# Group norm and attention on one core: the first input loaded, normalised and projected by channel chunks

## The chip, the cores and the metric

The kernel runs on one core of a Trainium2 chip. The metric is the device time of one execution in microseconds. "Span" is the length of the profiled execution; it is about 1.7 us shorter than the time of the same execution. PE is TensorE, DVE VectorE, ACT ScalarE, POOL GpSimd, SP SyncE.

## The reference

```python
# x: (4, 512, 48, 48) f32, 32 groups of 16 channels, 8 heads of 64
hn  = group_norm(x, gn_scale, gn_bias)                 # eps 1e-5
qkv = einsum('oc,bchw->bohw', qkv_w, hn) + qkv_b       # 1536 x 512, then f16
q, k, v = ...                                          # per head: 64 x 2304
w   = softmax(einsum('bhct,bhcs->bhts', q * s, k * s)) # s = 1 / sqrt(sqrt(64))
a   = einsum('bhts,bhcs->bhct', w, v)
out = x + einsum('oc,bchw->bohw', proj_w, a) + proj_b
```

## The kernel before

The 512 channels are four chunks c of 128 partitions; the 2304 positions are five blocks j, four of 512 and one of 256. A q or k chain of a head pair is, for one block, an accumulation over the four chunks. Each chunk is one step: two matmuls with 64 output rows, each of which the trace records as two passes (f32; 160 records for the 40 steps of pair 0). PE and DVE keep the order in which the program is written. The order of ACT, POOL and SP is chosen by the scheduler of the build. The front of the program, before attention starts:

```python
def load_x(b, j, engines):                   # block by block, all chunks of a block
    o, n = QBLOCKS[j]
    for c in range(NC):
        t = xpool.tile([P, n], F32, tag=f"x{c}_{j}", name=f"x_{b}_{c}_{j}")
        engines[c % len(engines)].dma_start(t, x[b, bass.ts(c, P), o : o + n])
        hn[b, c, j] = t
for j in range(NQ):
    load_x(0, j, (nc.sync, nc.scalar))
...
nc.gpsimd.dma_start(brow..., qkv_b[:, 2 * NC :]...)       # 512 values of 4 bytes
for part, engine in ((1, nc.sync), (0, nc.scalar), (2, nc.sync)):
    engine.dma_start(wqkv[:, :, cols], ...)               # 1 MB each
nc.gpsimd.partition_broadcast(bv, brow[0:1, :], P)        # bias of v on all partitions
...
nc.gpsimd.memset(gmat, 1.0 / GROUP)
for sign, base in ((1, 0), (-1, GROUP - 1)):
    nc.gpsimd.affine_select(out=gmat, in_=gmat, ...)      # gmat: 1/16 within a group
...
def group_mean(b):       # bn_aggr per chunk, PE: gmat x mean, DVE: mean, dev, dev^2, var
def group_var(b):        # PE: gmat x var; DVE: + eps; POOL: pow -0.5; DVE: ga, mga, gb
def norm(b, j):          # DVE: x * ga + gb, in place, per chunk
...
for j in range(NQ):
    stats(0, j)                              # DVE bn_stats
group_mean(0)
group_var(0)
norm(0, 0)
for j in range(NQ):
    if j + 1 < NQ:
        norm(0, j + 1)
    for part in (1, 0):                      # k chain, then q chain of block j
        for p in qk_chain(0, part, j):
            p[1]()
for i in range(0, NT, 2):                    # then the v chains, then attention
    for p in v_chain(0, 0, i):
        p[1]()
```

## Time and profile before

| | before |
|---|---|
| time, median of 4 runs | 1709.38 us (1708.64 to 1709.68) |
| span of the profiled execution (a run of 1708.11 us) | 1706.4 us |
| first q/k step on PE | 24.68 us |
| first v matmul on PE | 58.37 us |
| from there to the end | 1648.0 us |

After the first q/k step PE hardly rests any more. So the time of the first v matmul is the figure to watch: it contains all that the change touches. The prediction shows the views of this profile. In its chain of waits a piece is counted from the end of the one before, so v stands there at 58.53; PE's timeline has the start itself:

```profile
58.37 31.25 PE L712 MATMUL pv<-wqkv,x 128*64 128x256 f32 x288
```

The granted clock of this trace is on record from 30.18 on. It is 1.00 or 0.50 of full speed, and its nine changes after that lie whole multiples of 3.413 us apart (87 of them from 30.18 to 327.14, then two to 333.97). So windows of 3.41 us on that grid are used below, and "half clock" is a window at 0.50. Ahead of 30.18 the speed is read from the steps.

### The profile page before, as it was taken

What the parts mean: (1) busy time and instruction counts of PE and PEld (TensorE: products, weight loads), DVE (VectorE), ACT (ScalarE), POOL (GpSimd) and SP (SyncE); (2) the same over time, 40 slices, a digit from 0 to 9 for tenths busy, and PEclk for the clock granted to TensorE, in tenths of its full rate; (3) what the DMA queues carried; (4) which work ended last, traced back from release to release, by engine and by line L of the source; (5) the groups of instructions that cost most, each with busy time, mean ns of one, the idle gap of its engine ahead of it and who ended that gap; (6) DMA issues with size and microseconds to landing.
All of it is one profiled execution on the core that took longest, in us unless ns stands there. A gap on an engine that the chain in (4) does not pass through costs nothing.

```text
span 1706.4 us, 28896 instructions
## 1 busy us (share of the span) xinstructions
PE 1631.4 (96%) x11876; PEld 719.9 (42%) x11876; DVE 1019.8 (60%) x1124; ACT 1232.9 (72%) x1297; POOL 345.0 (20%) x497
## 2 busy tenths in 40 slices
PE   4999999899999999899999999999999999999896
PEld 1533444254333543445433344355534334444344
DVE  5256555876555555767556555676655555566564
ACT  0077787767787786767787777876777888877882
POOL 1001112111211211231211211122111221123331
PEclk9999999999999999999999999999999999999999
DMA  6001002200000012430100001343010000024233
GB/s 204 1 19 26 11 15 77 64 8 17 14 11 13 17 26 73 141 101 18 48 14 10 14 17 22 100 132 95 14 44 11 14 17 14 14 78 115 69 106 114
DMA packets 93774, 81.89 MB, mean 48 GB/s; under 512 B 50880, under 2 KB 58944, under 8 KB 93632
## 3 DMA queue, kind: packets, MB, share of 16 engines
q1 hardware_dynamic: 91488, 76.51, 16.3%
q10 hardware_dynamic: 1968, 3.41, 0.6%
q8 instruction: 95, 1.56, 0.4%
q14 instruction: 47, 0.39, 0.1%
q0 software_dynamic: 176, 0.02, 0.0%
HBM read 60.44 MB, written 19.16 MB: 47 GB/s over the span
## 4 chain that ended last, share of the span: by engine, by line
PE 87%; DVE 5%; DMA 3%; ACT 3%; issue 2%; POOL 0%; SPq 0%; DVEq 0%; POOLq 0%; ACTq 0%
PE pqk L672 29%; PE ps L831 17%; PE av L856 17%; PE pv L712 14%; PE pr L760 7%; PE sl L904 3%; ACT p L838 3%; DVE acc L888 2%; DVE st L589 1%; DMA out_dram<-r 1%; DMA x<-x_dram 1%; DMA r<-x_dram 1%; DVE x L628 1%; DVE avx L865 0%; DMA ib<-row 0%
## 5 line engine op out<-in xcount | busy, mean ns | idle before, releaser
L838 ACT ACTIVATE p<-ps 128x1024 f16<-128x1024 f32 x1296 | 1231.6, 1027 | 427.5 <-PE ps L831 426.9
L672 PE MATMUL pqk<-x,wqkv 128*64 128x512 f32 (+1 forms) x2560 | 540.8, 555 | 6.1 <-DVE x L628 2.6
L888 DVE TENSOR_TENSOR acc<-acc,p 128x3072 f16<-128x3072 f16 x270 | 481.7, 1784 | 81.7 <-ACT p L838 81.0
L831 PE MATMUL ps<-q,k 64*128 64x512 f16 (+1 forms) x2880 | 364.4, 360 | 15.3 <-ACT p L838 14.9
L856 PE MATMUL av<-p,v 128*64 128x512 f16 (+1 forms) x2880 | 362.1, 365 | 0.1
L672 PEld LDWEIGHTS pqk<-x,wqkv 128*64 128x64 f32 x2560 | 176.4, 138 | 247.1 <-issue 188.2
L941 POOL TENSOR_SCALAR in<-sums 128x8 f32<-128x8 f32 (+1 forms) x160 | 115.0, 719 | 803.0 <-DMA sums<-slx 796.5
L712 PE MATMUL pv<-wqkv,x 128*64 128x256 f32 x2304 | 267.7, 380 | 1.4 <-DVE x L628 1.4
L831 PEld LDWEIGHTS <-k 64*128 64x128 f16 x2880 | 107.7, 94 | 291.6 <-issue 245.4
L856 PEld LDWEIGHTS <-v 128*64 128x64 f16 x2880 | 131.6, 109 | 212.4 <-issue 168.9
L963 POOL TENSOR_TENSOR att<-avx,ib 128x512 f16<-128x512 f32 (+1 forms) x78 | 119.8, 1536 | 421.5 <-DMA ib<-row 378.2
L712 PEld LDWEIGHTS pv<-wqkv,x 128*64 128x64 f32 x2304 | 160.0, 137 | 93.9 <-issue 7.2
L888 DVE TENSOR_TENSOR acc<-p,p 128x3072 f16<-128x3072 f16 x80 | 140.2, 1753 | 62.1 <-ACT p L838 61.6
L681 DVE TENSOR_SCALAR q<-pqk,bqkv 128x512 f16<-128x512 f32 (+1 forms) x80 | 55.8, 697 | 140.2 <-PE pqk L672 140.2
L720 DVE TENSOR_TENSOR v<-pv,bv 128x512 f16<-128x512 f32 x72 | 49.8, 691 | 135.5 <-PE pv L712 135.5
L681 DVE TENSOR_SCALAR k<-pqk,bqkv 128x512 f16<-128x512 f32 (+1 forms) x80 | 55.8, 697 | 125.0 <-PE pqk L672 125.0
L760 PE MATMUL pr<-a,whi 128*128 128x512 f32 (+1 forms) x304 | 121.0, 404 | 3.9 <-POOL a L752 3.3
L760 PE MATMUL pr<-a,wlo 128*128 128x512 f32 (+1 forms) x304 | 113.7, 380 | 0.0
L771 DVE SCALAR_TENSOR_TENSOR r<-pr,bproj,r 128x512 f32<-128x512 f32 (+1 forms) x80 | 55.3, 696 | 86.2 <-PE pr L760 75.6
L752 POOL CAST a<-att 128x512 fp32r<-128x512 f16 (+1 forms) x75 | 64.3, 891 | 88.0 <-PE pr L760 87.7
L904 PE MATMUL sl<-acc,ones 128*64 128x512 f16 (+1 forms) x576 | 67.4, 350 | 13.0 <-DVE avx L865 12.8
L760 PEld LDWEIGHTS pr<-a,whi 128*128 128x128 f32 x304 | 57.2, 188 | 41.6 <-issue 21.9
(56 smaller groups left out, 385.3 us busy)
## 6 DMA issues: line engine op xcount, KB each, us to landing
r<-x_dram SPq DMA_DIRECT2D x64, 256.0 KB, 2.9
out_dram<-r SPq DMA_DIRECT2D x64, 256.0 KB, 2.5
ib<-row SPq DMA_DIRECT2D x126, 128.0 KB, 3.0
x<-x_dram SPq DMA_DIRECT2D x56, 256.0 KB, 3.2
x<-x_dram ACTq DMA_DIRECT2D x8, 256.0 KB, 7.1
wqkv<-qkv_wT_dram SPq DMA_DIRECT2D x2, 1024.0 KB, 8.1
sums<-slx SPq DMA_DIRECT2D x128, 2.0 KB, 2.1
r<-x_dram SPq DMA_DIRECT2D x16, 128.0 KB, 2.2
```

The lines of the kernel that those rows point to most:

```text
L672: nc.tensor.matmul(pw[0][lo : lo + D, :n], wqkv[:, c, w0 + lo : w0 + lo + D], hn[b, c, j], start=(c == 0), stop=(c == NC - 1),)
L681: nc.vector.tensor_scalar(qk[g][part][:, o : o + n], pw[0][:, :n], bqkv[:, col : col + 1], SCALE, ALU.add, ALU.mult,)
L712: nc.tensor.matmul(pw[0][lo : lo + D, a, :], hn[b, c, i * P // QB][:, at + lo : at + lo + D], wqkv[:, c, 2 * C + half * C // 2 :][:, : C / ...
L752: engine.tensor_copy(at32[b, j][:, c, :n], atts[b * NPAIR + c][:, o : o + n])
L760: nc.tensor.matmul(ps[:, :n], w[:, c, bass.ts(m, P)], at32[b, j][:, c, :n], start=(c == 0 and i == 0), stop=(c == NC - 1 and i == 1),)
L831: nc.tensor.matmul(ps[:, h, a * n : (a + 1) * n], kt[rows, bass.ts(i, P)], qt[rows, o : o + n], start=True, stop=True,)
L838: nc.scalar.activation(pt[:, r], ps, AF.Exp)
L856: nc.tensor.matmul(av[0][lo : lo + D, :n], vv[b, pr // 2][:, i, pr % 2 * P + lo : pr % 2 * P + lo + D], pt[:, r, h, a * n : (a + 1) * n], ...
L888: nc.vector.tensor_tensor(acc[g, j][0], before, pt, ALU.add)
L904: nc.tensor.matmul(sl[lo : lo + D, :n], ones16, t[:, r, h, a * n : (a + 1) * n], start=(i == 0), stop=(i == len(steps) - 1),)
L941: nc.gpsimd.tensor_scalar(t, sm, limit, None, op)
L963: nc.gpsimd.tensor_tensor(atts[g][:, o : o + n], avx.pop((g, j))[:, :n], ib[:, :n], ALU.mult)
```

## The change

The intent: PE waits 24.7 us because the group norm is started only when all of x has arrived. Groups lie within a chunk, so a chunk's norm needs nothing of the other chunks. The change loads chunk 0 first and takes its statistics, coefficients and norm. It then carries six open accumulation chains (five k, one q, in six PSUM banks) one step forward with each chunk. The norm of the first x goes to ScalarE, the bias broadcast is written further down, and small slices of the k and q weights are loaded ahead.

```diff
+    load_w(1, slice(0, P), nc.scalar)
+    for c in range(NC):
+        for j in range(NQ):
+            load_x(0, j, c, (nc.sync, nc.scalar)[j % 2])
+        if c == 0:
+            load_w(0, slice(0, P), nc.scalar)
+    load_w(2, slice(0, C), nc.sync)
+    load_w(1, slice(P, C), nc.scalar)
+    load_w(0, slice(P, C), nc.sync)
 ...
+    bv = const.tile([P, C], F32, name="bv")              # was above gmat
+    nc.gpsimd.partition_broadcast(bv, brow[0:1, :], P)
 ...
+    def norm_chunk(b, c):
+        ga, gb = coef["ga", b], coef["gb", b]
+        for j in range(NQ):
+            t = hn[b, c, j]
+            nc.scalar.activation(
+                t, t, AF.Identity, bias=gb[:, c : c + 1], scale=ga[:, c : c + 1]
+            )
 ...
+    def coefficients(c):
+        for j in range(NQ):
+            stats(0, j, (c,))
+        group_mean(0, (c,))
+    six = [(1, j) for j in range(NQ)] + [(0, 0)]
+    banks = [
+        ps_s.tile([P, 2, QB], F32, tag="ps", name=f"ps_{i}") for i in range(3)
+    ]
+    chains = [qk_steps(0, *a, banks[i // 2][:, i % 2, :]) for i, a in enumerate(six)]
+    coefficients(0)
+    group_var(0, (0,))
+    for c in range(NC):
+        norm_chunk(0, c)
+        for i, step in enumerate(chains):
+            step(c)
+            if c + 1 < NC and i == 1:
+                coefficients(c + 1)
+            if c + 1 < NC and i == 3:
+                group_var(0, (c + 1,))
+    for j in range(1, NQ):                               # the other four q chains
+        for p in qk_chain(0, 0, j):
+            p[1]()
```

The cuts: group mean and variance take a list of chunks and write columns of shared tiles; qk_steps is the body of qk_chain with a bank given from outside.

## The prediction

> **What bounds the kernel now.** I read the page first (busy shares, slices, chain), then the chain of waits and the timeline of the first 80 us, because the change touches nothing after that. TensorE is busy for 96% of the 1706.4 us span. The only long stretch without it is the front: the first of 40 slices shows PE at 4 tenths, all others at 8 or more. So the front is worth about 24.7 us, and after it PE's order fixes the rest: a microsecond gained or lost before PE turns continuous should move the end by about one.
>
> The page's busy line and two rows of the slices:
>
> ```profile
> PE 1631.4 (96%) x11876; PEld 719.9 (42%) x11876; DVE 1019.8 (60%) x1124; ACT 1232.9 (72%) x1297; POOL 345.0 (20%) x497
> ...
> PE   4999999899999999899999999999999999999896
> ...
> PEclk9999999999999999999999999999999999999999
> ```
>
> The chain of waits, cut to 0 to 80 us (start, duration, what):
>
> ```profile
> 2.18 7.71 DMA x<-x_dram
> ...
> 9.90 6.80 DMA x<-x_dram
> ...
> 16.73 2.59 DVE st L589 x6
> 19.32 0.65 DVE mv L594 x4
> ...
> 20.11 0.57 PE gmean L596 x2
> ...
> 22.39 1.07 POOL rstd L614
> ...
> 24.68 33.85 PE pqk L672 x160
> 58.53 21.58 PE pv L712 x199
> ```
>
> Read it so: x arrives until 16.7, the last statistics end at 19.3, the group coefficients take from 20.11 to 24.05, one norm 0.6, then PE has 33.85 us of q/k chains for pair 0 and goes on with v at about 58.45. That last time is what the change has to beat.
>
> The timeline of GpSimd shows something the chain does not, as it is hidden in before:
>
> ```profile
> 5.64 0.37 POOL L552 TENSOR_SCALAR_AFFINE_SELECT gmat<-gmat 128x128 f32<-128x128 f32 x1 [0.28 <-POOL fine L570]
> 13.18 0.80 POOL L529 PARTITION_BROADCAST bv<-brow  x1 [7.17 <-DMA brow<-qkv_b_dram]
> 13.84 0.46 POOL L552 TENSOR_SCALAR_AFFINE_SELECT gmat<-gmat 128x128 f32<-128x128 f32 x1
> ```
>
> The group matrix gmat is finished at 14.30 only, because its second select stands behind the broadcast of a bias row whose load lands at 13.1. Every group mean needs gmat.
>
> Last, PE's busy time in windows of 3.41 us (columns: window, its length, PE busy, PEld, DVE, ACT, POOL, PE clock, DMA, GB/s):
>
> ```profile
> 323.73:327.14 3.41, 1.55 (x10) 0.55 (x10) 3.31 (x4) 3.41 (x5) 0.00 (x0) 1.00 0.18 53
> 327.14:330.55 3.41, 2.00 (x10) 0.69 (x11) 3.41 (x6) 0.29 (x1) 0.00 (x0) 0.50 0.00 0
> 330.55:333.97 3.42, 3.34 (x18) 0.91 (x12) 2.69 (x7) 3.24 (x4) 0.00 (x0) 0.50 0.04 1
> 374.93:378.34 3.41, 1.85 (x22) 1.03 (x23) 2.20 (x3) 0.65 (x1) 0.00 (x0) 1.00 0.02 5
> ```
>
> I laid these windows over the whole span: four with PE busy for 0.84 to 1.60 us were followed by half clock, none with 1.85 or more was (the end aside). Half clock ended after a window of 3.34 or 3.41 us busy, and did not end after one of 2.00.
>
> [...] the first six 512-column steps (two 64-row halves, two passes each) come every 1.71 us, the later ones every 0.857, turning at 30.2, though the page's clock row prints 9 there. [...] here 47% busy was already too little. [...] Before's table load is 1.28 us; no norm runs on ScalarE in before[...]. [...] the bias row, 512 values of 4 bytes: 8.6 us to landing, and 592 packets under 512 B in the first 70 us.
>
> **The change part by part.** I compared the two built programs instruction by instruction on each engine.
>
> (1) Loads. x comes chunk by chunk, with small slices of the k and q weights ahead. No byte less. Each load waits for the one eight places earlier (before: SP waited 9.7 us for x). Chunk 0 lies in the first six loads; before's first eight were in by about 10 us, so its statistics end near 9. That gains nothing, since gmat comes at 14.3: **the source moves the broadcast down, but GpSimd's built order still has it ahead of the second select.** The first group mean runs at about 14.35 instead of 20.11. Its coefficients need 24.05 - 20.11 = 3.93 us, as before (waits and fixed costs, not columns): 18.28.
>
> (2) The norm of the first x goes from VectorE to ScalarE. 20 norms (16 of 0.48 and 4 of 0.34 us pitch, 9 us) leave VectorE, all beside PE. ScalarE gets 20[...]. But ScalarE issues 12 loads first; its last waits for the 15th. In before the third weight load was gated alike and was issued at 17.3. Table load 1.28: ScalarE is free at about 18.6. [...] **PE starts at about 19.4 instead of 24.68, 5.3 us earlier.**
>
> (3) PE's work is the same: ten chains, 8 x 3.43 + 2 x 1.72 = 30.9 us warm. It is only cut: six chains (5.5 steps of 0.857 = 4.7 us per chunk) run in four portions, four q chains follow unbroken (3 x 3.43 + 1.72 = 12.0). Three more pairs of tiny group matmuls (0.6 us each, cold) come in.
>
> (4) New waits: VectorE works in order, and the code puts the statistics of chunk c+1 after the coefficients of c, group mean after PE step 2, group variance after step 4. So a loop of dependences forms, per chunk: statistics 4 x 0.638 + 0.33 = 2.88, aggregate 0.2, group mean until PE goes on about 0.5, two PE steps 1.71, variance to coefficients 24.04 - 21.51 = 2.53. Sum **7.8 us per chunk, against 4.7 us of PE work**. PE waits about 0.5 us before the mean and 1.5 us before the next chunk; the rest is tiny matmuls.
>
> Sum: chunk 0 starts at 19.4. It is cold: 3.43 + 0.6, two steps partly cold 2.6, 2.53[...] make 9.9, so chunk 1 starts at about 29.3 or, where the clock turns early, 28.5. Two rounds of 7.8: chunk 3 at 44.5 (28.5 to 29.3 + 15.6). Its steps 4.7, then 12.0: v starts at about **61.4 against 58.45, 3 us later**. The head start of 5.3 is spent: in the loop PE idles or does tiny matmuls for about 9 us, and cold steps still cost 2 to 3 us as before.
>
> (5) Clock. In the loop a 3.41 us window that catches both pauses has 1.7 us of PE work, next to the 1.60 that throttled and the 1.85 that did not. A trip costs up to 1.7 us, some of it hidden in the pauses. I add 1 us. After the front nothing differs: later batches keep VectorE norms and the same pools.
>
> **Rivals.** A, the intent works: PE starts 5 us earlier and stays fed, v starts at 53 to 54, time 1704 to 1705. For it: the loads and ScalarE are fast enough. Against: the statistics of the next chunk stand behind this one's coefficients. I give it 7%. B, my loop with a warm clock: 1711 to 1714, 55%. C, loop plus throttling once or twice: 1714 to 1717, 23%. D, PE never warms in the loop, as its pauses keep every window below what ends half clock: a chunk costs 10.7 us, v starts 10 to 12 us late, 1720 to 1722. For it: 61% busy did not wake it in before. Against: cold, PE would be over 80% busy. 12%. E, gmat or ScalarE's start moves by 2 us with the bias row's or the 15th load's landing: it shifts B or C by 1 to 2 us. Small rest: something unseen.
>
> **Range and chances.** The middle of B and C is 1709.55 + 3 + 1 = 1713.5 us. Below, A alone goes under 1709; above, D ends near 1721. The three runs before span 1 us. A range from 1709.0 to 1719.5 should hold it 8 times in 10. Two per cent is 34 us, more than the whole front before PE starts: same 0.985, faster 0.005, slower 0.01.
>
> **What would show it.** gmat's second select near 14.3 behind the broadcast; the first group mean just after; ScalarE's first norm near 18.6 after the table load; first q/k matmul near 19.4; statistics of each chunk starting right after the coefficients of the one before; chunk starts 7.8 us apart; v from about 61.4. I am wrong if the second q/k portion starts within 6 us of the first (A), if steps stay at 1.71 us past 35 us (D), or if PE's pauses after 62 us change.

## The result

The changed kernel takes 1718.96 us (median of 4 runs, 1718.32 to 1721.22), 9.6 us more than before. A ratio, here and below, is the mean time of one kernel's fast runs over that of the other's of the same rounds, so it is not quite the ratio of the medians: 1.0059, 95% interval 1.0042 to 1.0076. By the 2% measure that is "same". In the trace the first v matmul moved from 58.37 to 68.91 us, 10.5 us, and the span grew by 10.7; from there to the end it is 1648.2 us against 1648.0. So all of the loss lies in the front.

The page's busy line and the slices of PE:

```profile
PE 1636.3 (95%) x11888; PEld 722.4 (42%) x11888; DVE 1014.9 (59%) x1128; ACT 1246.6 (73%) x1317; POOL 343.3 (20%) x500
...
PE   4999999899999999989999999999999999999796
```

At this scale nothing is to be seen: the first slice is 4 tenths as before. ACT has gained 20 norms (13.7 us). The chain of waits, cut to 0 to 80 us, tells more (start, duration, what):

```profile
3.80 8.94 DMA brow<-qkv_b_dram
...
14.05 0.60 PE gmean L617 x2
...
16.27 5.65 issue
21.92 0.60 POOL rstd L635
...
23.12 0.82 ACT x L654
...
23.99 3.68 PE ps L698 x8
...
32.35 2.72 DVE st L602 x5
...
39.41 2.72 DVE st L602 x5
```

The loads of x have left the chain, as intended, and the first group mean runs at 14.05 instead of 20.11. Then 5.65 us pass in which the chain shows "issue", that is, no releaser that the profile knows, before GpSimd's power. So the first q/k step starts at 23.99, only 0.7 us earlier than before. After that, up to the last chunk, the chain goes through VectorE's statistics for each chunk, not through PE.

GpSimd's timeline of the changed kernel (in brackets the idle time before, and its end):

```profile
13.54 0.46 POOL L560 TENSOR_SCALAR_AFFINE_SELECT gmat<-gmat 128x128 f32<-128x128 f32 x1
21.92 0.59 POOL L635 TENSOR_TENSOR rstd<-veps,mhalf 128x1 f32<-128x1 f32 x1 [7.92 <-issue]
```

The power's input was there at 16.26, and GpSimd had been idle since 14.00. The packed trace holds two MODIFY_POOL_CONFIG records at 13.92 and 13.96, between the two lines (the views of the profile leave them out), and two more at 5.97 and 6.00, ahead of the broadcast. What GpSimd does in this hole no instruction of the profile shows. In before the same records stand at 14.23 and 14.26 and the same gap of 8.09 us stood ahead of the power, but there VectorE's input ended it (22.30, power at 22.39), so the profile named VectorE and the hole did not show.

PE's timeline, the starts of chunks 1 and 2, the last chunk and v, then its busy time in two clock windows (columns as in the prediction):

```profile
33.25 1.94 PE L698 MATMUL ps<-x,wqkv 128*64 128x512 f32 x8 [0.88 <-ACT x L654]
...
40.31 1.94 PE L698 MATMUL ps<-x,wqkv 128*64 128x512 f32 x8 [0.87 <-ACT x L654]
...
47.37 1.08 PE L698 MATMUL ps<-x,wqkv 128*64 128x512 f32 x4 [0.87 <-ACT x L654]
49.39 3.33 PE L698 MATMUL ps<-x,wqkv 128*64 128x512 f32 x8 [0.95 <-DVE k L707]
53.66 1.51 PE L698 MATMUL ps<-x,wqkv 128*64 128x512 f32 x8 [0.94 <-DVE k L707]
55.98 1.08 PE L698 MATMUL ps<-x,wqkv 128*64 128x512 f32 x4 [0.80 <-DVE k L707]
...
68.91 21.32 PE L743 MATMUL pv<-wqkv,x 128*64 128x256 f32 x196
```

```profile
46.37:49.79 3.42, 1.60 (x8) 0.42 (x8) 0.84 (x2) 3.29 (x5) 0.00 (x0) 1.00 0.01 2
49.79:53.20 3.41, 2.93 (x8) 0.60 (x4) 1.19 (x2) 0.13 (x1) 0.00 (x0) 0.50 0.00 0
```

Chunks 1, 2 and 3 start 7.06 us apart. In the last one PE waits three times 0.8 to 0.95 us for VectorE, which reads a finished k chain out of PSUM. The window with the wait for ScalarE at the chunk's start and the first of these three has 1.60 of 3.42 us of PE work, and the next one runs at half clock: the step pair after 49.39 takes 3.33 us instead of 1.94 (in e5 the same pair, after the same wait, takes 1.94).

### The profile page after: what moved, and what is told of

It is laid out like the page before. It is cut to its first block, busy times and chain, and to the rows that moved or that the text cites. A ratio compares the mean times of both kernels' runs of the same rounds, so it can differ in the third digit from the quotient of the medians.

```text
span 1717.1 us, 28955 instructions
## 1 busy us (share of the span) xinstructions
PE 1636.3 (95%) x11888; PEld 722.4 (42%) x11888; DVE 1014.9 (59%) x1128; ACT 1246.6 (73%) x1317; POOL 343.3 (20%) x500
## 4 chain that ended last, share of the span: by engine, by line
PE 87%; DVE 5%; ACT 2%; DMA 2%; issue 2%; POOL 1%; SPq 0%; DVEq 0%; ACTq 0%; POOLq 0%
PE pqk L698 27%; PE ps L862 17%; PE av L887 17%; PE pv L743 14%; PE pr L791 7%; PE sl L935 3%; ACT p L869 2%; DVE acc L919 2%; DVE st L602 1%; PE ps L698 1%; DMA r<-x_dram 1%; DMA out_dram<-r 1%; DMA brow<-qkv_b_dram 1%; DVE x L645 0%; DVE avx L896 0%
## 5 line engine op out<-in xcount | busy, mean ns | idle before, releaser
L698 PE MATMUL pqk<-x,wqkv 128*64 128x512 f32 (+1 forms) x2464 | 518.1, 551 | 3.3 <-DVE k L707 2.0
L698 PEld LDWEIGHTS pqk<-x,wqkv 128*64 128x64 f32 x2464 | 168.9, 137 | 229.6 <-issue 177.2
L919 DVE TENSOR_TENSOR acc<-p,p 128x3072 f16<-128x3072 f16 x80 | 140.3, 1753 | 61.4 <-ACT p L869 60.8
L707 DVE TENSOR_SCALAR k<-pqk,bqkv 128x512 f16<-128x512 f32 (+1 forms) x75 | 52.3, 697 | 114.7 <-PE pqk L698 114.7
```

Of the source, the lines that this page charges most:

```text
L698: nc.tensor.matmul(pw[0][lo : lo + D, :n], wqkv[:, c, w0 + lo : w0 + lo + D], hn[b, c, j], start=(c == 0), stop=(c == NC - 1),)
L707: nc.vector.tensor_scalar(qk[g][part][:, o : o + n], pw[0][:, :n], bqkv[:, col : col + 1], SCALE, ALU.add, ALU.mult,)
L919: nc.vector.tensor_tensor(acc[g, j][0], before, pt, ALU.add)
```

## The experiments

The theory after the trace: three causes, each in the front. (F) GpSimd's hole between the broadcast and the first power (7.92 us after the second select, 5.65 of them with the input there) sets the start. (S) VectorE's order, with the statistics of a chunk behind the coefficients of the one before, sets the distance of the chunks. (W) In the last chunk PE waits for the reader of the neighbour bank, and the clock drops. The rivals: ScalarE's norms, the loads, or the chunk-wise form itself.

All eleven kernels (there is no e6 on record) gave results that agree with the reference. "First step" and "first v" are from the profiled execution of each; times are medians. The runs of before beside each call had medians of 1710.44, 1710.91, 1710.29 and 1709.96 us (11 runs each).

| kernel | first step | first v | time us | ratio to before (95%) |
|---|---|---|---|---|
| before | 24.68 | 58.37 | 1709.38 | |
| the change | 23.99 | 68.91 | 1718.96 | 1.0059 (1.0042 to 1.0076) |
| e1_bias_dma | 19.18 | 61.93 | 1713.87 | 1.0022 (1.0010 to 1.0034) |
| e2_last_order | 24.97 | 64.96 | 1716.48 | 1.0038 (1.0025 to 1.0051) |
| e3_ahead | 24.96 | 62.82 | 1713.04 | 1.0018 (1.0006 to 1.0031) |
| e4_norm_dve | 25.05 | 75.02 | 1726.97 | 1.0096 (1.0082 to 1.0111) |
| e5_block_loads | 24.41 | 67.40 | 1718.78 | 1.0044 (1.0031 to 1.0057) |
| e7_reordered | 14.21 | 53.08 | 1704.66 | 0.9964 (0.9950 to 0.9977) |
| e9_reordered_warm | 16.75 | 52.56 | 1706.43 | 0.9968 (0.9954 to 0.9982) |
| e8_before_warm | 29.30 | 60.27 | 1707.66 | 0.9981 (0.9968 to 0.9995) |
| e10_before_warm_short | 27.96 | 61.81 | 1708.92 | 0.9980 (0.9964 to 0.9996) |
| e11_before_bias_dma | 24.30 | 58.25 | 1711.07 | 1.0007 (0.9995 to 1.0020) |
| e12_before_bias_warm | 26.02 | 56.99 | 1706.74 | 0.9989 (0.9975 to 1.0004) |

### e1_bias_dma: no broadcast on GpSimd

```diff
-    nc.gpsimd.partition_broadcast(bv, brow[0:1, :], P)
+    browd = dram.tile([1, C], F32, tag="browd", bufs=1, name="browd")
+    nc.sync.dma_start(browd, brow)
+    nc.sync.dma_start(bv, browd.to_broadcast((P, C)))
```

> The changed kernel, but the bias row is spread over the partitions by two small loads instead of GpSimd's broadcast[...]. Theory L (the 5.65 us hole before the first power, 16.27 to 21.92,[...]): the hole is gone, gmat is ready near 6.2, the first coefficients near 13.8, and then ScalarE's loads and table set the start: first norm near 18.9, first q/k step near 19.8 instead of 24.0, total 4 us less, about 1715. Rival (GpSimd is slow there for another reason, for instance the traffic of the loads): the power still starts after 20 and the total stays near 1719.

GpSimd's timeline of this kernel:

```profile
5.30 0.77 POOL L560 TENSOR_SCALAR_AFFINE_SELECT gmat<-gmat 128x128 f32<-128x128 f32 x2
12.02 0.58 POOL L637 TENSOR_TENSOR rstd<-veps,mhalf 128x1 f32<-128x1 f32 x1 [5.95 <-DVE veps L636]
```

Both selects run together at 5.30, and the power follows its input at once (0.08 us after it). Its trace holds MODIFY_POOL_CONFIG records at 5.20 and 5.23 only, none between the selects and the power. The loads of x and weights are the same, so the rival falls. That the broadcast makes the hole, cause F, is shown; what GpSimd does in it is not. The start moved to 19.18, not to 13, because ScalarE first issues its eleven loads: its table load began at 17.02 and its first norm at 18.32. The gain was 1.0059 to 1.0022, about 6 us, more than the expected 4: in this execution the clock was warm at 22.7 already and didn't drop in the last chunk.

### e2_last_order: the last chunk's steps in another order

```diff
-        for i, step in enumerate(chains):
-            step(c)
+        last = c + 1 == NC
+        for i in (0, 2, 4, 1, 3, 5) if last else range(6):
+            chains[i](c)
```

> The changed kernel, but in the last chunk the six steps run in the order 0, 2, 4, 1, 3, 5, so that no step follows at once the step of the other half of its two-bank tile. Theory W (in the last chunk PE waits for VectorE's read of the neighbour bank, 0.9 us three times, and these pauses bring the half clock at 49.8): the three waits go, 2.7 us, and with them the half-clock window, 1.7 us; v starts 3 to 4.5 us earlier than 68.9, total 1714.5 to 1716. Rival (the waits are for VectorE's throughput and only move): the same waits at the later steps, total within 1 us of 1719.

PE's timeline in the last chunk:

```profile
47.27 1.08 PE L698 MATMUL ps<-x,wqkv 128*64 128x512 f32 x4 [0.86 <-ACT x L654]
48.68 4.42 PE L698 MATMUL ps<-x,wqkv 128*64 128x512 f32 x20 [0.33 <-ACT x L654]
```

The three waits for VectorE are gone, one of 0.33 us for ScalarE is new, and the clock holds. It holds in e1, e3 and e5 too, which keep the three waits, so the waits alone do not bring the half clock; that it depends on how the pauses lie in the windows is argued, not shown. The portion takes 47.27 to 52.93, 5.7 us, where it took 47.37 to 56.89, 9.5 us, in the change, and 47.25 to 55.38, 8.1 us, in e5, in the change's order but at full clock. So the order was worth 2.4 us and the half clock 1.4. First v comes 3.9 us earlier, within the expected 3 to 4.5; the total at 1716.48 is half a microsecond above the expected range. The intervals of e2 and of the change overlap, so the gain in total time is not settled; the gain in the trace is. The steps of a pair write different banks; the wait comes from the two banks being one tile in the program. That reading is argued from the order of waits in the build; shown is that the waits go when the steps of one tile don't follow each other.

### e3_ahead: statistics and coefficients ahead on VectorE

```diff
-    coefficients(0)
-    group_var(0, (0,))
+    for c in (0, 1): chunk statistics                  # shortened
+    for c in (0, 1): group_mean(0, (c,))
+    group_var(0, (0,), (0,))                           # up to the power
+    for c in (2, 3): chunk statistics
+    group_var(0, (0,), (1,))                           # ga, mga, gb
+    group_var(0, (1,))
 ...
-            if c + 1 < NC and i == 1:
-                coefficients(c + 1)
-            if c + 1 < NC and i == 3:
-                group_var(0, (c + 1,))
+            if c + 2 < NC and i == 1:
+                group_mean(0, (c + 2,))
+            if c + 2 < NC and i == 3:
+                group_var(0, (c + 2,))
```

> The changed kernel, but VectorE's order is turned: all statistics are taken before the first coefficients are finished, and the coefficients run one chunk ahead of the steps. Theory S (the loop statistics, mean, two steps, variance, coefficients, norm sets the chunk distance of 7.1 us, not the loads, not ScalarE, not PE): chunks follow each other every 5.1 to 5.5 us, the start stays at 24.0, v starts near 62 to 63, total 1712 to 1714. Rival (ScalarE's norms or the loads set the distance): it stays at 7 us and the total near 1719.

PE's timeline, from the end of chunk 0 to the start of chunk 3:

```profile
31.01 3.23 PE L701 MATMUL ps<-x,wqkv 128*64 128x256 f32 x16
34.16 0.38 PE L617 MATMUL gmean<-mv,gmat 128*128 128x1 f32 x2
...
36.66 7.09 PE L701 MATMUL ps<-x,wqkv 128*64 128x256 f32 x36
```

No idle time stands before any of them: PE goes from one chunk into the next. The same point of two neighbouring chunks lies 5.65 us apart (31.01 and 36.66), against 7.06 in the change (40.31 less 33.25); expected were 5.1 to 5.5, a little less. Cause S is shown, and ScalarE's norms and the loads, which are as in the change, do not set the distance. GpSimd's hole (8.67 us ahead of the power) and the bank waits (0.95, 0.94 and 0.81 us) are still there.

### e4_norm_dve: the norm stays on VectorE

```diff
-            nc.scalar.activation(
-                t, t, AF.Identity, bias=gb[:, c : c + 1], scale=ga[:, c : c + 1]
-            )
+            nc.vector.tensor_scalar(
+                t, t, ga[:, c : c + 1], gb[:, c : c + 1], ALU.mult, ALU.add
+            )
```

> The changed kernel, but the norm of the first x stays on VectorE as it was before. By theory S VectorE's queue is in the loop, so 2.2 us of norms ahead of the next statistics lengthen each warm chunk from 7.1 to about 9.1 us and the cold one by about 1: v 5 to 7 us later than 68.9, total 1724 to 1728, more where the clock drops. Rival (ScalarE's slower norm, 0.82 against 0.54 us, is what costs): 1 to 3 us faster, total 1716 to 1718.

The first q/k steps of chunks 1 and 2, and the group mean between them, on PE's timeline:

```profile
34.39 1.94 PE L698 MATMUL ps<-x,wqkv 128*64 128x512 f32 x8 [0.61 <-DVE x L654]
39.12 0.38 PE L617 MATMUL gmean<-mv,gmat 128*128 128x1 f32 x2 [2.79 <-DVE mv L615]
...
43.72 1.94 PE L698 MATMUL ps<-x,wqkv 128*64 128x512 f32 x8 [0.60 <-DVE x L654]
```

VectorE's norm hands over faster (0.60 against 0.87 us), but the chunk distance is 9.33 us (expected 9.1), as the next statistics come 2.2 us later: PE waits 2.79 us for the mean. The total is 1726.97, as theory S expected. So moving the norm to ScalarE was worth about 6 us of first v to the change (75.02 against 68.91).

### e5_block_loads: x by blocks again

```diff
-    for c in range(NC):
-        for j in range(NQ):
-            load_x(0, j, c, (nc.sync, nc.scalar)[j % 2])
-        if c == 0:
+    for j in range(NQ):
+        for c in range(NC):
+            load_x(0, j, c, (nc.sync, nc.scalar)[c % 2])
+        if j == 0:
             load_w(0, slice(0, P), nc.scalar)
```

> The changed kernel, but the first x is loaded block by block again (the small weight slices stay ahead). Theory N (the loads by chunk buy nothing as the change stands[...]): chunk 0 is complete near 16.5 instead of 7.4, the first group mean comes 2 to 3 us later than 14.05, the first power and the first q/k step stay within 1 us of 21.9 and 24.0, total within 2 us of 1719. Rival (the head start rests on the loads): first step near 27, total 1721 to 1723.

GpSimd's and PE's timeline:

```profile
13.53 0.80 POOL L582 PARTITION_BROADCAST bv<-brow  x1 [7.52 <-issue]
...
18.29 0.56 PE L617 MATMUL gmean<-mv,gmat 128*128 128x1 f32 x2 [18.29 <-DVE mv L615]
...
24.41 3.68 PE L698 MATMUL ps<-x,wqkv 128*64 128x512 f32 x8 [4.14 <-ACT x L654]
...
49.28 1.94 PE L698 MATMUL ps<-x,wqkv 128*64 128x512 f32 x8 [0.95 <-DVE k L707]
```

The first mean is 4.2 us later than in the change (expected 2 to 3) and the first step 0.4 us later; the totals don't differ (the intervals overlap). As the change stands, its title part, the loads by chunk, buys nothing. The first line adds one thing: here the bias row had landed (8.6 us after its issue) before 13.53, and the broadcast still began only 7.5 us after the select, with no releaser named. GpSimd has a hole ahead of the broadcast as well, so gmat's late end, which the prediction put down to the landing of the bias row, is due to that hole at least in this run. The last line is the pair of steps after the first wait for VectorE: the wait is there as in the change, the window with it has 1.74 us of PE work, and the clock does not fall.

### e7_reordered: the three causes removed together

The edits of e1 and e2; all first loads issued by SP, so that ScalarE only loads its table; and VectorE's and PE's order as follows.

```diff
+    chunk_stats(0); group_mean(0, (0,)); group_var(0, (0,)); chunk_stats(1)
+    for c in range(NC):
+        norm_chunk(0, c)
+        # group mean of c + 1: after step 1 in chunk 0, else ahead of the steps,
+        #   followed on VectorE by the statistics of c + 2
+        # group variance of c + 1: after step 3 in chunk 0, else after step 1
```

> All repairs together: bias row by loads, all first loads issued by SP so that ScalarE is free, statistics one chunk ahead of the coefficients on VectorE, the group matmuls of the next chunk ahead of the steps, last chunk in the order 0, 2, 4, 1, 3, 5. If the three causes found are the whole of it ([...]VectorE's order, the bank waits), the first q/k step comes near 14.2, v starts near 53 instead of 58.4 (before) and 68.9 (change): total 1703 to 1706, faster than both. Rival (the chunk-wise form itself costs, for instance its small group matmuls and the cold clock): v after 56, total 1707 or more.

PE's timeline, the first chunk and the later part:

```profile
14.21 3.40 PE L700 MATMUL ps<-x,wqkv 128*64 128x512 f32 x8 [2.35 <-ACT x L656]
...
23.59 3.30 PE L700 MATMUL ps<-x,wqkv 128*64 128x512 f32 x8 [0.26 <-ACT x L656]
...
33.02 8.21 PE L700 MATMUL ps<-x,wqkv 128*64 128x512 f32 x40
```

First step at 14.21 (expected 14.2), first v at 53.08 (expected near 53), total 1704.66: 0.36% faster than before (by the 2% measure still "same") and faster than the change. Removing the three causes, together with ScalarE's eleven issues, takes away the whole loss of 10.5 us of first v and 5.3 us more. All of them were removed at once, so this run does not say what each is worth in it. One pause of 1.4 us for the second mean, at 21.5, remained and cost a half-clock window from 24.02.

### e8, e9 and e10: throw-away matmuls for the clock

In before the first steps run at half speed until 30.2 (1.71 us each, later ones 0.857). These kernels put 128-column matmuls on gmat, whose result nobody reads, into PE's wait. e8: 26 + 4 + 12 of them around the two group matmuls of before. e9: 18 + 4 + 12 in e7. e10: 13 + 2 + 7 in before.

```diff
+    warm(26)        # e10: 13
     group_mean(0)
+    warm(4)         # 2
     group_var(0)
+    warm(12)        # 7
     norm(0, 0)
```

> The kernel before, with 42 throw-away 128-column matmuls on gmat between 14.3 and the first q/k step; the result is not used. It measures what the cold clock at the first steps costs by itself: in before the steps ran at 1.71 us until 30.2, 5.5 us of cold work. If PE is warm by 24.7, v starts near 55.6 instead of 58.4, total 2 to 3 us less than before; if the windows do not count such short matmuls, no change.

> The reordered kernel with 34 such throw-away matmuls ahead of its first step, from 6.2 us on. If they warm the clock: v another 1.5 to 3 us earlier than in the reordered kernel, total 1701 to 1704. If the clock falls back in the pauses around the first group matmuls, no gain.

> The kernel before with 22 throw-away matmuls in place of 42. In the trace of the longer version such a matmul took about 0.38 us cold and 0.245 warm, so that 26 of them ran to 23.5 and pushed the first group mean 3.4 us back. 13 cold ones from gmat at 14.3 to 15.2 end near 20, when the mean is due; 7 fill the wait for the power and the first norm. If PE is warm by then, steps come every 0.857 from the start, q/k takes about 31 us instead of 33.85, v starts 1 to 3 us before 58.4, total 1 to 3 us less than before; if the pauses in the coefficients put the clock back or never wake it, the first steps take 1.71 us and the total equals before within 1 us.

My sizes were off in e8 and e9: such a matmul took longer than I had allowed for. In e8's trace they start 0.427 us apart cold and 0.223 us warm (the 0.38 and 0.245 in the expectation of e10 are not these distances). So the throw-away work ran past the group mean's turn (to 23.5 in e8, to 12.4 in e9), and the start came 4.6 and 2.5 us later. In e8 the late group matmuls make 3.2 us of that (the one for the variance at 24.72 against 21.51); the rest is GpSimd's power, which began at 27.02 though its input was there at 25.21. The steps themselves were warm: in e8 the chains took 31.1 us instead of 33.85. In e10 the size was right (the mean at 20.43), but GpSimd's power came late. Its lines in e8 and e10:

```profile
27.02 1.05 POOL L614 TENSOR_TENSOR rstd<-veps,mhalf 128x4 f32<-128x4 f32 x1 [11.36 <-issue]
```

```profile
25.68 1.05 POOL L614 TENSOR_TENSOR rstd<-veps,mhalf 128x4 f32<-128x4 f32 x1 [10.74 <-issue]
```

PE then waited 4.35 us in e10, the clock fell back at 26.95, and the chains were cold again (34.0 us). e9 gained nothing measurable over e7. The totals of e8 and e10 are 0.2% below before although their first v is later in the profiled execution. In both the time after the first v is shorter than before's by 1 to 2 us, with 10.2 us (e8) and 13.7 us (e10) at half clock instead of 17.1 (the last windows of the span aside); whether the throw-away work has to do with that is open.

### e11 and e12: before without the broadcast, cold and warm

e11 is before with the bias edit of e1. e12 adds 8 + 2 + 7 throw-away matmuls that read an x tile instead of gmat, so that they begin when that tile lands.

> The kernel before with the bias row spread by two small loads in place of GpSimd's broadcast. In before's trace the first power waited for VectorE (veps at 22.30) and began at 22.39, about 8.1 us after the second select[...]. Theory H (hidden as a rule): the first power still begins near 22.4, the first q/k step near 24.7, total within 1 us of before. Theory O (often on the path in before as well, with more in its slower runs): total 1 to 3 us less than before.

> The same, with 17 throw-away matmuls that read an x tile that lands near 16.7, so that they run from there to the first q/k step. [...]nothing should keep PE waiting for over 2 us after them. If the clock is warm by the first step, the q/k chains take about 31 us instead of 33.85 and v starts near 55.6: total 2 to 3 us less than the version without them. If they don't wake the clock, equal to it.

The chains in e11 and e12 on PE's timeline:

```profile
24.30 34.12 PE L674 MATMUL pqk<-x,wqkv 128*64 128x512 f32 x160 [2.56 <-DVE x L630]
```

```profile
26.02 31.14 PE L674 MATMUL pqk<-x,wqkv 128*64 128x512 f32 x160 [0.89 <-DVE x L630]
```

e11 equals before: the hole was hidden there, theory H. In e11 the power began at 22.03, 0.08 us after its input, in before at 22.39, 0.09 us after it and 8.09 us after the second select. Where the profile names no releaser for the power, the hole took 7.7 (e5) to 11.4 us (e8); that in before it was hidden only just is an estimate from these. That is why it could be overlooked. e12 measures the cold start by itself: the same 160 passes take 3.0 us less when warm. The start is 1.7 us later, since the tile landed at 18.47 and not near 16.7, so first v comes 1.3 us earlier in the trace. In time e12 is faster than e11 by the medians (1706.74 against 1711.07), but the two intervals overlap; the gain in time is not settled.

## Why the prediction was right or wrong

The time, 1718.96 us, lies in the range of 1709.0 to 1719.5, near its upper end; "same" had 0.985. The middle, 1713.5, was 5.5 us too low. It lies between rival C (up to 1717) and rival D (from 1720), so none of the rivals describes it. By the prediction's own steps:

1. "The source moves the broadcast down, but GpSimd's built order still has it ahead of the second select": right. gmat was finished at 14.00 (predicted 14.3), the first mean ran at 14.05.
2. "Its coefficients need 24.05 - 20.11 = 3.93 us, as before": **this step failed.** They took from 14.05 to 23.09, 9.0 us. In before GpSimd's hole (8.09 us) ran in the shade of the loads; brought forward by 6 us, the chain met it. e1 removes it and the chain takes about 3.5 us again (9.76 to 13.2; VectorE's small steps take 0.16 us on one column as on four, the power 0.58 instead of 1.06). The sign for it was in before's profile: the power began 8.1 us after the second select, and only the releaser's name said VectorE. The first step was predicted at 19.4 and came at 23.99: +4.6 us.
3. ScalarE free "at about 18.6": right, 18.88 (it issues eleven loads, not 12). With the late power it did not matter; in e1 it set the start. The prediction's times for a norm on ScalarE were my estimate, as no trace had shown one there; in the trace of the change the five of a chunk take 3.42 us, the first 0.82 to its hand-over.
4. The loop: right in kind (e3, e4), a little too long in size. Predicted 7.8 us per chunk, measured 7.06. The terms that were too large: variance to coefficients, 2.53 against 1.8 us (37.62 to 39.4), as the power of one column takes 0.55 us instead of 1.06 and the warm variance matmul 0.33 instead of 0.6. Chunk 3 started 23.4 us after chunk 0, predicted 25.1: -1.7 us.
5. The last chunk, "its steps 4.7": **failed.** It took 9.5 us. I took the steps to be free of VectorE, but three of them wait for the reader of the neighbour bank (2.7 us), and in this execution the clock fell to half (1.4 us, against e5); what the remaining 0.7 us are was not traced, but e2, which brings the portion to 5.7, still waits for ScalarE's tiles. +4.8 us.
6. The clock: right in number, wrong in place. Rival C was a trip or two in the pauses of the loop; its windows from 29.31 to 46.37 held at least 2.40 us of PE work and none tripped. The one trip came in the last chunk, after a window of 1.60 us, through waits that the prediction did not have. That it cost about the 1 us set aside is luck. A reading was off too: in before, three steps ran at 1.71 us, not six (24.68 to 30.18 is 5.5 us; it is six halves of a step).
7. Rival D, a clock cold through the loop, was the nearest above the measured time but did not happen: the clock woke at 29.3, during chunk 0. Rival A did not happen either; e7 shows what it needs.

The sum of the differences, +4.6 - 1.7 + 4.8 = +7.7, is the 7.5 us between the predicted first v, 61.4, and the measured 68.9 (the prediction's terms add up to 61.2). The time came out 5.5 us above the middle, since the 1 us set aside for the clock is in this sum; the last 1 us is within the scatter of the runs. That the range held is in part luck: two costs of nearly 5 us each were missing from the prediction, and without the 1.7 us by which the loop was shorter the time would have come out near 1720.7, above the range.

## What to carry to other kernels

A wait that is hidden today is the next bound when the work above it moves forward: before predicting such a move, look at what each engine did just ahead of the moved instruction, not only at the releaser that is named. When a long phase is cut into portions, write down the loop of dependences through the engine that works in order; here VectorE's order cost more than the earlier data gave (chunk 1's statistics began at 23.01 in the change, right behind chunk 0's coefficients; in e3 they had ended at 14.65). And where PE's work becomes thin, add up its busy time in windows of 3.4 us: in these runs a window with less than 1.4 us of PE work was always followed by one at half clock, one with 1.42 to 1.81 us sometimes, one with 1.84 us or more never.

## What the traces of all thirteen kernels add

- Windows and clock: laid over the profiled executions of all thirteen kernels, windows with 1.42 to 1.81 us of PE work went either way: 1.60 (before and the change, once each), 1.75 (e7) and 1.81 (e12) were followed by half clock, 1.42 (the change) and 1.74 (e5) were not. Once the clock was up, all windows with less than 1.42 were, and none with 1.84 or more. To wake it took more: 2.67 (the change) did not, 2.79 (e4) and all above did. Some records of matmuls can be missing, so these are not sharp limits.
- Half clock in mid-kernel differs between executions: the last chunk with its three waits lost 1.4 us to it in the change and nothing in e1, e3 and e5. How much of the scatter between runs of one kernel is due to it is open: the part after the first v matmul is the same work and took 1646.1 to 1652.5 us in the thirteen profiled executions; the two with 20.5 us of half clock in it are the longest (1652.0 in e3, 1652.5 in e9), among the eleven with 10.2 to 17.1 us no order is to be seen.
- GpSimd's hole: the power began 1.9 us after its input in e5 and 5.65 us after it in the change. From the second MODIFY_POOL_CONFIG record to the power it took 7.7 us (e5), 8.0 (the change), 9.0 (e2), 10.8 (e10) and 11.4 (e8); why it varies is open. No instruction of the profile stands in it: the profile prints "issue", or another releaser where that came later. With a broadcast over partitions between the two selects there were two holes, one ahead of the broadcast (7.52 in e5) and one ahead of the power; without it (e1) the selects ran together and the power followed its input.
- Short f32 matmuls with their weight loads, of 128 columns and 128 x 128 weights, start 0.427 us apart cold and 0.223 us apart warm (e8).
